# A planned two-block transformer kernel: linear attention rewritten around shifted weights, causal maxima taken four heads at a time, and the instruction order stored as a table

## The chip, the cores and the metric

The kernel runs on one core of one Trainium2 chip. The metric is device time in microseconds (us) of one launch. The host only lays the arrays out. Five engines work in parallel: TensorE (PE in the profile, with its weight loads as PEld), VectorE (DVE), ScalarE (ACT), GpSimd (POOL) and SyncE (SP), which issues the DMAs. Each runs its own instructions in order and waits on semaphores for the others. TensorE and the engines exchange results through PSUM (eight banks of 512 fp32 columns in this kernel); GpSimd is used on SBUF alone here.

## The reference

Eight sequences of 512 rows and 128 features pass four sublayers, each behind a layer norm without weights and each added to its input. Cut to what matters:

```python
x = x + L0_attn(layernorm(x))      # linear attention, 16 heads of 64, elementwise form
x = x + L0_ffn(layernorm(x))       # SwiGLU with blockwise FP4 rounding of x, h and the weights
x = x + L1_attn(layernorm(x))      # causal softmax attention, 16 heads of 8
x = x + L1_ffn(layernorm(x))       # RMS norm, top 2 of 8 LoRA experts on shared weights

def L0_attn(x):
    q, k, v = x @ wq + bq, x @ wk + bk, x @ wv + bv      # (8, 512, 16, 64) each
    Q, K = elu(q) + 1, elu(k) + 1
    KV   = sum over s of K * v                           # one number per batch, head, feature
    Ksum = sum over s of K
    attn = Q * KV / (Q * Ksum + 1e-6)
    return gelu(attn @ wo + bo)

def L1_attn(x):                
    a = (q @ k.T) / sqrt(8);  a = where(causal mask, a, -max)
    return softmax(a) @ v @ Wout
```

All arithmetic is fp32 (the expert masks are bf16, exact).

## The kernel before, in words

`block_kernel` (L745) doesn't issue instructions directly. Every call on the proxy engines is recorded as a `Step` by `Engine.__getattr__` (the lambda around L537 leads to `Plan.add`, L190), and issued at the end from `Plan.issue`. That is why nearly every row of the profile has one line, L407: it is the `getattr(e, method)(*a, **k)` in `issue`. Groups are told apart by the names of their tiles (`ahead`, `pair`, `mid` are PSUM; `kf`, `qf`, `z`, `r`, `act`, `qa`, `pr`, `mx` and so on are SBUF).

`Plan.ordered` (L249) chooses the order: a list scheduler on an estimate of each step's cost, with ranks from the table `TURNS` (one pair of numbers for each stage of each lane: loads, norm, linear, out, fp4, attention, routing, experts). A step marked `either` goes to GpSimd or VectorE, whichever the scheduler finds free first. `Plan.kept_warm` (L365) puts filler matmuls on `zeros` into gaps that the plan shows on TensorE. Sequences overlap: while one is in attention and experts, the next ones are in linear attention and the feed-forward.

Each sequence goes through these stages, with the features in 128-row chunks and the 512 rows as columns:

- `linear_attention` (L978). For each of eight chunks of 128 features, `features` (L993) makes k, v and q with one fp32 matmul of 512 columns each. `elu` (L982) adds the bias by ScalarE twice, once in a Relu into SBUF and once in an Exp in place in PSUM, then VectorE takes `min(exp - 1, relu)` and, for k, the sum `ks`. So `kf` and `qf` hold elu without the 1, which is added later: to `ks` by a one-element step, to `qf` by an Identity with bias `one_sb`. VectorE multiplies k by v (`kv`), ScalarE makes `z = q * ks + eps` and scales the chunk of `wo` (`wk_o`). `products` (L1015) handles chunks in pairs, so that one reciprocal `r` of `z0 * z1` serves two: five products on `either`, two reciprocals of 256 columns on VectorE.
- `linear_out` (L1031): eight accumulated matmuls `wk_o` by `qf`, GELU, transposes, residual.
- `fp4_feed_forward` (L1100) with `quantised` (L1054): a chain of reductions, products and bit operations on VectorE and `either`.
- `causal_attention` (L1336): four groups of four heads for each sequence, 32 in all, in `group` (L1286). The scores are taken transposed, so the row maxima must be known first. `largest` (L1210) makes the maxima of the next group, query block by query block (t = 0 to 3, with 128, 256, 384, 512 keys): matmuls of q by k for two heads in row strips 0 to 31 and 64 to 95 of TensorE, a mask added by bf16 matmuls of `mask_q` by the identity, and one VectorE reduction over 512 to 1024 elements. `to_queries` (L1236) sends the maxima as two extra rows into the q tile, `scores` (L1255) multiplies with them, ScalarE exponentiates, GpSimd masks the diagonal block, and four matmuls in column strips multiply by v (`va`) into `mid`.
- `routed` (L1356) and `experts` (L1428): 24 matmuls of 512 columns into pairs of `ahead` tiles, tanh on ScalarE, two VectorE steps, one product on `either`, then the down projection.

PSUM is two pairs of banks (`pair`), one `mid`, three `ahead`; an `ahead` tile may also take half of a pair while another pair stays open.

Of the kernel before, what the change touches and what calls it, by code (L numbers as in the profile page):

```python
# [9 lines left out]
F32 = mybir.dt.float32  # L10
F32R = mybir.dt.float32r
BF16 = mybir.dt.bfloat16
U32 = mybir.dt.uint32
AF = mybir.ActivationFunctionType
# [97 lines left out]
class Buf:  # L112


    def __init__(self, tag=None, place=None):
        self.tag, self.place = tag, place
        self.writer, self.readers = None, []
        self.first, self.users = None, {}


class Step:


    def __init__(self, number, engine, lane):
        self.number, self.engine, self.rank, self.lane = number, engine, 0.0, lane
        self.calls, self.needs, self.takes, self.uses = [], {}, [], {}
        self.cost, self.slow, self.port, self.size = 0.0, 0.0, False, 0
        self.work = 0.0
        self.start = self.end = None


TWO_PORTS = ("tensor_tensor", "scalar_tensor_tensor", "tensor_scalar", "tensor_copy")


class Plan:
# [3 lines left out]
    HOP = {"tensor": 0.1, "gpsimd": 0.1, "vector": 0.1, "scalar": 0.1, "sync": 0.2}  # L139

    def __init__(self, nc):
        self.nc, self.steps, self.open = nc, [], None
        self.lane, self.tags, self.psum, self.warmer = None, {}, (), None
        self.parts = {}
        self.engines = {n: Engine(self, n) for n in (*self.HOP, "either")}


    def tag(self, name, places, parts=None):

        self.tags[name] = list(places)  # L150
        self.parts[name] = parts or [((name, i),) for i in range(len(places))]
# [24 lines left out]

    def fixed(self, place):
        return View(Buf(place=place), place.shape)

# [4 lines left out]
    def together(self):  # L184
        return Together(self)

    def span(self, lane, low, high):
        return Span(self, lane, low, high)

    def add(self, engine, method, a, k):  # L190
        step = self.open
        if step is None:
            step = Step(len(self.steps), engine, self.lane)
            self.steps.append(step)
        elif step.engine is None:
            step.engine = engine
        assert step.engine == engine
        out = [k["out"]] if "out" in k else [a[0]]
        ins = [x for x in (*a[0 if "out" in k else 1 :], *k.values()) if isinstance(x, View)]
        if k.get("accum_out") is not None:  # L200
            out.append(k["accum_out"])
        step.calls.append((method, a, k))
        fast = "vector" if engine == "either" else engine
        if method is not None:
            step.cost += cost(fast, method, out[0], ins, a, k)
        if engine == "tensor" and method is not None:
            step.work += work(method, ins, a, k)
        if engine == "sync":
            step.size += 4 * out[0].shape[0] * _free(out[0])
        if engine == "either":  # L210
            step.slow += cost("gpsimd", method, out[0], ins, a, k)

        if engine == "gpsimd" and method != "memset":
            step.port = True
        elif engine in ("vector", "either") and method in TWO_PORTS:
            two = sum(v.shape[-1:] != (1,) or len(v.shape) > 2 for v in ins) > 1
            step.port |= (two or _free(out[0]) > 16) and not any(
                v.buf.tag in self.psum for v in (*ins, out[0]) if isinstance(v, View)
            )
        for v in ins:  # L220
            if all(v is not o for o in out) and isinstance(v, View):
                self.reads(step, v.buf)
        for v in out:
            if isinstance(v, View):
                self.writes(step, v.buf)

    def reads(self, step, buf):
        assert buf.writer is not None or buf.tag is None
        if buf.writer is not None and buf.writer is not step:
            step.needs[buf.writer] = True  # L230
        buf.readers.append(step)
        self.used(step, buf)

    def writes(self, step, buf):
        for s in (buf.writer, *buf.readers):
            if s is not None and s is not step:
                step.needs[s] = True
        buf.writer, buf.readers = step, []
        if buf.first is None and buf.tag is not None:
            buf.first = step  # L240
            step.takes.append(buf)
        self.used(step, buf)

    def used(self, step, buf):
        buf.users[step] = True
        step.uses[buf] = True


    def ordered(self):  # L249

        free = Free(self.parts)
        slots = {}
        left = {s: len(s.needs) for s in self.steps}
        then = {s: [] for s in self.steps}
        for s in self.steps:
            for n in s.needs:
                then[n].append(s)
        users = {}  # L260
        for s in self.steps:
            for b in s.uses:
                users[b] = len(b.users)
        ready_at = {s: 0.0 for s in self.steps}
        empties = set()
        for s in self.steps:
            for b in s.uses:
                if b.tag in self.psum and s.engine != "tensor" and (False or max(b.users, key=lambda u: u.number) is s):
                    empties.add(s)
        waiting = {e: [] for e in self.engines}  # L270
        for s in self.steps:
            if not left[s]:
                waiting[s.engine].append(s)
        turns = {}
        for s in sorted(self.steps, key=lambda s: (s.rank, s.number), reverse=True):
            for b in s.takes:
                turns.setdefault((s.lane, b.tag), []).append(b)
        busy = dict.fromkeys(self.engines, 0.0)
        port = 0.0
        moved = 0.0  # L280
        ends = []
        now, done, order, stuck = 0.0, 0, [], False
        clock = Clock()
        while done < len(self.steps):
            for e in self.HOP:
                while busy[e] <= now:
                    best, kept = None, set()
                    shared = waiting["either"] if e in ("vector", "gpsimd") else []
                    ready = [s for s in (*waiting[e], *shared) if ready_at[s] <= now]
                    ahead = HURRY if e == "tensor" and clock.idle(now) else 0.0  # L290
                    for s in sorted(
                        ready,
                        key=lambda s: (s.rank - (ahead if s.work > 0.6 * s.cost else 0.0) - (EMPTY if s in empties else 0.0), s.number),
                    ):
                        if s.port and port > now:
                            continue
                        asked = {}
                        for b in s.takes:
                            asked.setdefault(b.tag, []).append(b)
                        if not all(  # L300
                            all(b in turns[s.lane, t][-len(bs) :] for b in bs)
                            for t, bs in asked.items()
                        ):
                            continue
                        if all(
                            (t not in kept or stuck) and free.has(t, len(bs)) for t, bs in asked.items()
                        ):
                            best = s
                            break

                        kept.update(asked)
                    if best is None:
                        break
                    if any(
                        now < ready_at[s] <= now + PATIENCE and s.rank < min(best.rank - MARGIN, LIMIT)
                        for s in (*waiting[e], *shared)
                    ):
                        break
                    s, stuck = best, False
                    waiting[s.engine].remove(s)  # L320
                    if s.engine == "either":
                        s.engine = e
                        s.cost = s.slow if e == "gpsimd" else s.cost
                    for b in s.takes:
                        slots[b] = free.take(b.tag)
                        turns[s.lane, b.tag].remove(b)
# [1255 lines left out]
```

## Time and profile before

| what | before |
|---|---|
| median of 3 runs (lowest, highest) | 1126.88 us (1125.94, 1127.14) |
| the profiled execution: its span from first to last instruction | 1130.1 us |
| TensorE busy, granted clock | 1040.2 us, 0.982 in the mean |
| VectorE, ScalarE, GpSimd busy | 830.3, 630.8, 624.3 us |
| instructions TensorE, VectorE, ScalarE, GpSimd | 5025, 1868, 1084, 669 |
| first attention matmul, last group's output | 172 us, 1065 us |
| filler matmuls on `zeros` | 40.4 us busy |
| DMA | 44.3 MB, 11.9% of 16 engines |

The page gives no time of the profiled execution other than its span. It is 0.3% above the median of the runs, so a time worked out from the profile is multiplied by 1126.88 / 1130.1. An fp32 matmul stands as two records in the profile. "Busy" for TensorE is the union of records whose ends are modelled and overlap the next start: a matmul of 512 columns has a record of 0.5 to 0.6 us where the next starts 0.43 us later. GpSimd, VectorE and ScalarE records overlap the next one by some 0.05 to 0.1 us too. All work that the plan marked `either` ran on GpSimd in the kernel before.

### The profile page before, as it was taken

What the parts mean: (1) busy time and instruction counts of PE and PEld (TensorE: products, weight loads), DVE (VectorE), ACT (ScalarE), POOL (GpSimd) and SP (SyncE); (2) the same over time, 40 slices, a digit from 0 to 9 for tenths busy, and PEclk for the clock granted to TensorE, in tenths of its full rate; (3) what the DMA queues carried; (4) which work ended last, traced back from release to release, by engine and by line L of the source; (5) the groups of instructions that cost most, each with busy time, mean ns of one, the idle gap of its engine ahead of it and who ended that gap; (6) DMA issues with size and microseconds to landing.
All of it is one profiled execution on the core that took longest, in us unless ns stands there. A gap on an engine that the chain in (4) does not pass through costs nothing.

```text
span 1130.1 us, 15043 instructions
## 1 busy us (share of the span) xinstructions
PE 1040.2 (92%) x5025; PEld 488.0 (43%) x5025; DVE 830.3 (73%) x1868; ACT 630.8 (56%) x1084; POOL 624.3 (55%) x669
## 2 busy tenths in 40 slices
PE   6667788998899999999998999999999999999998
PEld 2223333344344444444543444454454445445454
DVE  6868879897888967758788968788667765556543
ACT  5756787678786644644578555764443443344311
POOL 6647846676676466237635755467644533441534
PEclk9879989999999999999999999999999999999999
DMA  8000030001101020111012000210002102001000
GB/s 235 1 1 0 1 111 1 21 20 56 39 20 30 10 94 20 58 72 35 26 39 94 19 21 20 95 30 19 20 7 98 39 20 104 21 20 30 1 10 9
DMA packets 30572, 44.31 MB, mean 39 GB/s; under 512 B 4192, under 2 KB 18464, under 8 KB 30496
## 3 DMA queue, kind: packets, MB, share of 16 engines
q1 hardware_dynamic: 30496, 43.37, 11.9%
q8 instruction: 39, 0.64, 0.2%
q14 instruction: 37, 0.30, 0.1%
HBM read 23.95 MB, written 18.87 MB: 38 GB/s over the span
## 4 chain that ended last, share of the span: by engine, by line
PE 57%; DVE 15%; ACT 6%; issue 2%; POOL 1%; DMA 0%; POOLq 0%; DVEq 0%; ACTq 0%
PE ahead L407 31%; PE pair L407 19%; PE mid L407 7%; ACT pr L407 2%; DVE r L407 2%; DVE mx L407 2%; DVE h L407 1%; DVE sc L407 1%; ACT qf L407 1%; DVE s4 routing L407 1%; DVE qf L407 1%; DVE act L407 1%; ACT z L407 1%; DVE kf L407 1%; DVE oh L407 1%
## 5 line engine op out<-in xcount | busy, mean ns | idle before, releaser
L407 ACT ACTIVATE pr<-pair 128x1024 f32<-128x1024 f32 (+1 forms) x192 | 166.7, 879 | 149.2 <-PE pair L407 129.1
L407 DVE TENSOR_REDUCE mx<-pair 128x4 f32<-128x512 f32 (+2 forms) x192 | 198.5, 1041 | 68.4 <-PE pair L407 57.7
L407 POOL TENSOR_SCALAR_AFFINE_SELECT pr<-pr 128x256 f32<-128x256 f32 (+1 forms) x192 | 92.8, 485 | 176.4 <-ACT pr L407 175.6
L407 PE MATMUL pair<-qkT 32*128 32x128 f32 (+7 forms) x1024 | 172.3, 387 | 9.4 <-ACT pr L407 2.7
L407 PEld LDWEIGHTS pair<-qkT 32*128 32x128 f32 (+1 forms) x1024 | 84.4, 183 | 181.8 <-ACT pr L407 52.0
L407 POOL TENSOR_TENSOR act<-act,tw 128x512 f32<-128x512 f32 x64 | 81.3, 1272 | 88.8 <-DVE act L407 80.6
L407 PE MATMUL ahead<-um,b_sb 128*128 128x512 f32 x240 | 122.2, 607 | 0.0
L407 DVE RECIPROCAL r<-r 128x256 f32<-128x256 f32 x64 | 110.3, 1736 | 14.9 <-POOL r L407 14.8
L407 DVE SCALAR_TENSOR_TENSOR act<-act,ahead 128x512 f32<-128x512 f32 x120 | 81.9, 684 | 51.4 <-ACT act L407 38.0
L407 POOL TENSOR_TENSOR qa<-qa,qa 128x704 f32<-128x704 f32 (+4 forms) x60 | 81.2, 1354 | 35.1 <-DVE qa L407 26.2
L407 POOL TENSOR_TENSOR qf<-qf,r 128x512 f32<-128x512 f32 x64 | 80.5, 1278 | 34.5 <-DVE r L407 27.8
L407 PE MATMUL mid<-pr,va 128*10 128x512 f32 (+3 forms) x1024 | 93.3, 435 | 0.0
L407 POOL TENSOR_TENSOR qf<-qf,z 128x512 f32<-128x512 f32 x64 | 80.3, 1270 | 0.0
L407 ACT ACTIVATE act<-ahead 128x512 f32<-128x512 f32 x60 | 35.8, 597 | 72.0 <-PE ahead L407 71.9
L407 PE MATMUL ahead<-act,a_sb 128*128 128x512 f32 x128 | 65.2, 619 | 0.0
L407 POOL TENSOR_TENSOR r<-z,z 128x512 f32<-128x512 f32 x32 | 40.9, 1278 | 41.6 <-ACT z L407 39.3
L407 PE MATMUL ahead<-tT,w_sb 128*128 128x512 f32 x120 | 63.3, 609 | 0.0
L407 ACT ACTIVATE ahead<-ahead,bqkv_sb 128x512 f32<-128x512 f32 x96 | 63.0, 656 | 0.0
L407 PE MATMUL pair<-mask_q,ident 128*128 128x128 bf16 (+1 forms) x384 | 61.6, 242 | 0.0
L407 PE MATMUL ahead<-xnT,wk 128*128 128x512 f32 x100 | 56.7, 650 | 4.8 <-DVE kf L407 2.1
L407 PEld LDWEIGHTS ahead<-um,b_sb 128*128 128x128 f32 x240 | 40.7, 190 | 36.1 <-issue 29.6
L407 ACT ACTIVATE z<-qf,eps_sb,s 128x512 f32<-128x512 f32 x64 | 51.9, 811 | 6.8 <-DVE s L407 5.1
(227 smaller groups left out, 1986.4 us busy)
## 6 DMA issues: line engine op xcount, KB each, us to landing
stacks<-qk SPq DMA_DIRECT2D x32, 512.0 KB
qkT<-stacks SPq DMA_DIRECT2D x128, 128.0 KB
x<-in SPq DMA_DIRECT2D x8, 256.0 KB
qkT<-mr SPq DMA_DIRECT2D x128, 4.0 KB
out<-x SPq DMA_DIRECT2D x8, 256.0 KB
w_sb<-in SPq DMA_DIRECT2D x3, 256.0 KB
wq<-in SPq DMA_DIRECT2D x4, 128.0 KB
wk<-in SPq DMA_DIRECT2D x4, 128.0 KB
```

Of the source, the lines that this page charges most:

```text
L407: getattr(e, method)(*a, **k)
```

## The change

Five parts go together.

1. *Order as a table.* `Step` and `Plan` lose costs, ranks and the scheduler; `issue` reads the order of all steps from a string `ORDER`, the engine of each `either` step from `ENGINES` (147 on VectorE, 229 on GpSimd), the buffer of each tile from `PLACES`, and twelve filler matmuls from `ZEROS`. PSUM is three pairs, one `mid`, one `ahead`, and an `ahead` tile may be any half of a pair. Some pools change their number of buffers.
2. *Biases and the 1 in shifted weights.* The last feature of a layer norm's output follows from the other 127, so that row of `xnT` is set to 1 (by the scale and bias of the copy out of PSUM), and twelve matmuls at the start make weights whose last row carries the bias, plus 1 for q and k. The projections then come out of TensorE with the bias and the 1 in them.
3. *One Exp a projection.* `elu + 1` is `max(p, min(exp(p - 1), 1))`: for k one Exp and one VectorE step (which also sums), for q one Exp and two VectorE steps.
4. *Quotient as kv/ks less a small term.* `Q KV / (Q ks + eps)` is `KV/ks * (1 - eps / (Q ks + eps))`. The first factor goes into `wk_o`, now on VectorE. The second is a reciprocal of `z`, taken for four chunks at once: nine products on `either` and two reciprocals of 256 columns for four chunks.
5. *Four-head maxima and mask factors.* The four heads of a group lie in the four row strips of TensorE; the causal mask is a product of two 32-row bf16 factors (`causal_factors`), also in four strips. Query blocks 0 and 1 share a step. The maxima of the two i-parts need one more tiny minimum, and `scores` takes 64 rows instead of 34 for one of the parts.

```diff
-    places("pair", [P, 2, 512], 2, pool=sums)
+    places("pair", [P, 2, 512], 3, pool=sums)
     places("mid", [P, 512], 1, pool=sums)
-    places("ahead", [P, 512], 3, pool=sums)
+    places("ahead", [P, 512], 1, pool=sums)
...
-    def issue(self):
-        for s in self.ordered():
+    def issue(self, order, engines, places, zeros):
+        engine = iter(engines)
+        for s in self.steps:
+            if s.engine == "either":
+                s.engine = {"v": "vector", "g": "gpsimd"}[next(engine)]
...
+        for at, n in enumerate(numbers):
+            s = self.steps[n]
             for b in s.takes:
-                b.place = self.tags[b.tag][self.slots[b]]
+                b.place = self.tags[b.tag][int(next(place), 36)]
+            if at in zeros:
+                self.warmer(zeros[at])
             e = getattr(self.nc, s.engine)
...
+    def shifted_weights():
+        nc.vector.tensor_scalar(
+            shift_b[:, 31, 0:16], bqkv_sb[:, 0:2].rearrange("p i c -> p (i c)"), 1.0, None, ALU.add
+        )
+        nc.vector.tensor_copy(shift_b[:, 31, 16:24], bqkv_sb[:, 2])
+        for part in range(4):
+            for i in (1, 2, 0):
+                w = wqkv[i][part]
+                pw = new("ahead", [P, 256])
+                with one_go():
+                    nc.tensor.matmul(pw, shift, w, start=True, stop=False, skip_group_check=True)
+                    for j in range(2):
+                        nc.tensor.matmul(
+                            pw[96:128, ts(j, P)], shift_b[:, :, 8 * i + 2 * part + j], ident,
+                            start=False, stop=True, skip_group_check=True,
+                        )
+                nc.scalar.copy(w, pw)
...
-            nc.scalar.activation(f, pw, AF.Relu, bias=bias)
-            nc.scalar.activation(pw, pw, AF.Exp, bias=bias)
-            nc.vector.scalar_tensor_tensor(f, pw, -1.0, f, ALU.add, ALU.min, **accum)
...
+        def keys(c):
+            ks, kv, rk = (new("s1", [P, 1]) for _ in range(3))
+            pw = projection(1, c)
+            kf = new("kf", [P, S])
+            nc.scalar.activation(kf, pw, AF.Exp, bias=minus_sb)
+            nc.vector.scalar_tensor_tensor(kf, pw, 1.0, kf, ALU.max, ALU.min, accum_out=ks)
+            nc.vector.scalar_tensor_tensor(
+                kf, kf, 1.0, projection(2, c), ALU.mult, ALU.mult, accum_out=kv
+            )
+            nc.vector.tensor_scalar(rk, ks, 1e-30, None, ALU.max)
+            nc.vector.reciprocal(rk, rk)
+            wk_o = new("wk_o", [P, D])
+            nc.vector.tensor_scalar(
+                wk_o, wo_sb[c // 2][:, c % 2, :], kv, rk, ALU.mult, ALU.mult
+            )
+            return ks, wk_o
+
+        def denominator(c, ks):
+            pw = projection(0, c)
+            z = new("qf", [P, S])
+            nc.scalar.activation(z, pw, AF.Exp, bias=minus_sb)
+            nc.vector.tensor_scalar(z, z, -1.0, 0.0, ALU.add, ALU.min)
+            nc.vector.scalar_tensor_tensor(z, z, 1.0, pw, ALU.add, ALU.max)
+            nc.scalar.activation(z, z, AF.Identity, bias=eps_sb, scale=ks)
+            return z
...
-            (q0, z0, w0), (q1, z1, w1) = features(c), features(c + 1)
-            r = new("r", [P, S])
-            nc.either.tensor_tensor(r, z0, z1, ALU.mult)
-            nc.either.tensor_tensor(q0, q0, z1, ALU.mult)
-            nc.either.tensor_tensor(q1, q1, z0, ALU.mult)
+            ab, cd, r = (new("r", [P, S]) for _ in range(3))
+            nc.either.tensor_tensor(ab, zs[0], zs[1], ALU.mult)
+            nc.either.tensor_tensor(cd, zs[2], zs[3], ALU.mult)
+            nc.either.tensor_tensor(r, ab, cd, ALU.mult)
             for part in (slice(0, 256), slice(256, S)):
                 nc.vector.reciprocal(r[:, part], r[:, part])
-            nc.either.tensor_tensor(q0, q0, r, ALU.mult)
-            nc.either.tensor_tensor(q1, q1, r, ALU.mult)
+            nc.either.tensor_tensor(cd, cd, r, ALU.mult)
+            nc.either.tensor_tensor(ab, ab, r, ALU.mult)
+            for z, other in zip(zs, (cd, cd, ab, ab)):
+                nc.either.tensor_tensor(z, z, other, ALU.mult)
+                nc.scalar.activation(z, z, AF.Identity, scale=-1e-6, bias=one_sb)
...
-    def stack(h):
-        return slice(64 * h, 64 * h + 32)
+    def stack(i, h):
+        return slice(64 * h + 32 * i, 64 * h + 32 * i + 32)
...
     def largest(n, t, mx):
...
+        t = max(t, 1)
+        some = (1, 0) if t == 1 else (t,)
+        w = sum((u + 1) * P for u in some)
+        pairs = [new("pair", [P, 2, 512]) for _ in range(2)]
+        four = [(i, h) for h in range(2) for i in range(2)]
+        with one_go():
+            for u in some:
+                for i, h in four:
...
+                    nc.tensor.matmul(
+                        to, duo(n, i)[stack(i, h), 0, ts(u, P)], keys,
+                        start=(u == t), stop=False, skip_group_check=True,
+                    )
+            k = len(some)
+            for i, h in four:
+                nc.tensor.matmul(
+                    pairs[i][:, h, w - k * P : w].rearrange("p (k c) -> p k c", k=k),
+                    mask_q[stack(i, h)],
+                    mask_k[stack(i, h)].unsqueeze(1).to_broadcast([32, k, P]),
+                    start=False, stop=True, skip_group_check=True,
+                )
...
-                        rows = slice(64 * h, 64 * h + 34)
+                        rows = slice(64 * h, 64 * h + (64 if i else 34))
```

## The prediction

> **What bounds the kernel now.** I read the page first: busy time by engine, then the 40 slices.
>
> ```profile
> PE 1040.2 (92%) x5025; PEld 488.0 (43%) x5025; DVE 830.3 (73%) x1868; ACT 630.8 (56%) x1084; POOL 624.3 (55%) x669
> PE   6667788998899999999998999999999999999998
> DVE  6868879897888967758788968788667765556543
> ```
>
> TensorE leads, but not everywhere: in the first third VectorE is as busy as TensorE. So next I asked for busy time by stretch. I cut where the fourth and the 24th attention group write `on` (337.3 and 896.4 us), because both kernels pass these points with nearly the same work behind them. The columns are stretch, length, then busy time (and count) of PE, PEld, DVE, ACT, POOL, then the granted clock.
>
> ```profile
> 0.00:337.30 337.30, 276.34 (x1020) 122.45 (x1020) 272.78 (x659) 240.97 (x427) 220.85 (x239) 0.95 0.14 42
> 337.30:896.40 559.10, 540.25 (x2865) 257.57 (x2864) 429.12 (x944) 311.86 (x532) 315.61 (x333) 1.00 0.13 42
> 896.40:1130.10 233.70, 223.65 (x1143) 107.96 (x1142) 128.43 (x265) 77.93 (x126) 87.80 (x98) 0.99 0.09 28
> ```
>
> Stage A (337.3 us): VectorE 81% and TensorE 82%, and of TensorE's 276 us 24 are filler matmuls on `zeros`. Each of the four engines is filled to 65 to 82%, so waits between engines set the pace, with VectorE the one with least room. Stage B (559.1): TensorE 97%, VectorE 77%. Stage C (233.7): TensorE 96%. In B and C a microsecond taken from TensorE is a microsecond of the kernel until VectorE is full.
>
> Third, the groups by form: prices of what goes and what comes (busy, mean ns of one).
>
> ```profile
> L407 DVE RECIPROCAL r<-r 128x256 f32<-128x256 f32 x64 | 110.3, 1736 | 14.9 <-POOL r L407 14.8
> L407 DVE TENSOR_TENSOR x<-ahead,x 128x512 f32<-128x512 f32 x8 | 5.5, 690 | 3.3 <-PE ahead L407 3.3
> L407 DVE TENSOR_SCALAR y<-y 128x512 f32<-128x512 f32 x8 | 3.3, 417 | 2.2 <-ACT y L407 2.2
> L407 ACT ACTIVATE wk_o<-wo,s 128x128 f32<-128x128 f32 x64 | 25.1, 394 | 9.5 <-DVE s L407 6.3 <-PE ahead L407 3.1
> L407 POOL TENSOR_TENSOR qf<-qf,z 128x512 f32<-128x512 f32 x64 | 80.3, 1270 | 0.0
> ```
>
> Last, TensorE's timeline at a maxima step, since means of a pipelined engine overlap and only start-to-start times add up (start, length, instructions):
>
> ```profile
> 706.68 0.49 PE L407 MATMUL pair<-qkT 32*128 32x512 f32 x2
> 707.11 0.28 PE L407 MATMUL pair<-mask_q,ident 128*128 128x128 bf16 x2
> 707.32 0.62 PE L407 MATMUL mid<-pr,va 128*10 128x256 f32 x8
> ```
>
> Two heads' matmuls of 512 columns, in two row strips, take 0.43 us together (706.68 to 707.11). The two mask matmuls behind them take 0.21 here, 0.12 at most other places (66 and 56 ns from start to start).
>
> **The change, part by part.** The counts are from the built instruction orders of both kernels.
>
> *Maxima on TensorE.* Start-to-start times of a pair in the trace are 0.172, 0.211, 0.370 and 0.428 us for 128, 256, 384 and 512 columns. A group needs two pairs of each: 2.36 us. Its masks are eight of 128 columns (0.061 each) and four of 256 (0.115 each): 0.95 us. After, four heads stand in four strips and four banks. If four run in the time of two, the first term halves: 1.18 saved. The masks become 32-row matmuls in four strips: 0 to 0.71 saved, depending on whether the strips overlap. No row shows four row strips at once. The nearest is the attention-times-value step with four column strips, whose four matmuls start 6 to 7 ns apart, so I take overlap for the maxima and about half of it for the masks: 1.5 us a group, 48 us in all (bounds 0 and 60). VectorE's reductions stay at 192 instructions and 5120 elements a group (198.5 us): nothing there.
>
> A rule speaks for caution here. The Trainium skill, "TensorEngine Tiling (Array Packing)", section "PSUM Bottleneck", says that row tiling speeds up the matmul but not the copying out, which may then be the bottleneck. By it alone the maxima step would be worth nothing, because the reduction of 1.22 us for two heads is longer than the 0.64 us of matmuls before it. The row that decides is stage B, with TensorE at 97% and VectorE at 77%: other matmuls take the freed time.
>
> *Shifted weights.* Twelve times a 256-column fp32 matmul (half of the 0.86 of a 512-column one, 0.43), two of 128 (0.11 each) and a ScalarE copy of about 0.35: 8 us on TensorE, 4 on ScalarE, once, in stage A.
>
> *Linear attention on ScalarE.* 128 Relu of 685 ns go (-88), 64 `wk_o` scalings go (-25), 12 copies come: -108 us, 631 to about 523. The Identity behind the quotients takes the place of the one behind `qf`.
>
> *On VectorE.* 32 of 64 reciprocals go: -56. There come 64 tensor_scalar on `qf` at 417 (+27), 64 `wk_o` scalings, about 0.28 each by the 270 ns of the one-element row with two scalars (+18), 32 tiny minima and some 25 set-up steps (+12). The small `s` steps change by -5. And 147 tensor_tensor that all ran on POOL move over: 112 of 512 at 690 (+77), 25 of 704 at some 0.95 (+24), 10 smaller (+5). The sum is +102 by means; engine time is about 0.8 to 0.9 of means, because the next instruction starts some 80 ns before the last ends, so +82: 830 to 912. By place in the built order +20 fall in stage A, +33 in B, +28 in C.
>
> *On POOL.* 118 products of 512 go at 1.27 (-150), 35 longer or equal ones of `quantised` and ten smaller ones (-58): 624 to about 420.
>
> *Contention.* VectorE now has some 210 more instructions that read SBUF alone while POOL works there. The row: the eight `y<-y,y` on VectorE last 681 ns at least, 684 in the median and 1082 once, and the mean is 734. One in eight stretched by 0.4 us makes 210 x 0.05 = 10 us; all of them would be 84. I take +8 by that row, since POOL is busy two fifths of the time.
>
> The Trainium skill, "GPSIMD Engine Reference", section 8, "Key points", says that POOL shares its SBUF interfaces with VectorE and contends with two-input VectorE instructions, which speaks against moving products over. By it each moved product could be stretched; the one row in eight is what this trace shows.
>
> *Filler and clock.* 44 filler matmul steps become 12. They stand in gaps and are worth 0 to 6 us after stage A. Against that, the clock: in stage A the grant is 0.95, and fewer fillers could lower it. A grant of 0.90 would cost TensorE some 14 us in A, where it is not alone on the path: 0 to +10, taken at +2.
>
> *Order, PSUM.* The order at run time is now a table in the source. PSUM is three pairs and one single bank instead of two and three, and single tiles take half-pairs, so up to seven of them can be open. Where both orders pass the 4th and the 24th group, TensorE's need counted with the same prices differs by -3 in A, -44 in B and about 0 in C (where more of the experts' work now lies): -47 in all, which is -48 and fillers left out, +8 for the weights, and rounding between stages.
>
> **The sum**, against the profiled 1130.1 us. A: VectorE 273 + 20 = 293 busy; it was idle 64 us, waiting mostly on POOL and ScalarE (`r` 10.2, `kf` 10.0 us), which are 35 and 17% lighter; I take 37 idle: 330. B: 559 - 44 = 515, VectorE then at (429 + 33) / 515 = 90%, so I add 5 of new waits for it: 520. C: -2, a last stage with more free engines: 232. Together 1082. Runs stand to the profiled execution as 1126.88 to 1130.1, so 1079 us.
>
> **Rivals.** *Better packed*: with ScalarE and POOL light, VectorE idles only 20 us in A (313), TensorE's idle time in B halves from 19 (506) and C loses its 10 us of idle time (222): 1041, 1038 as run. For it: twelve fillers instead of 44, so the recorded order sees few gaps on TensorE. Against: VectorE would have to be over 91% busy in A and B, and its best 100 us so far were 88.
>
> *Strips that don't overlap four at a time*: only some of the masks' time is saved (B 548), with A 335 and C 236: 1119, 1116 as run. For it: no row shows four row strips. Against: the four column strips.
>
> *Slower: VectorE as the bound.* It decides if VectorE cannot be kept busy over 84% in A and B, where it now has 293 + 462 = 755 us (755 / 896). At the shares it had, 81% in A and 82% in the fullest late 100 us of B, A takes 362 and B 565: 1161, 1158 as run. For it: products and scalings move to the engine that had least room in A. Against: what it waited for in A is exactly what gets lighter.
>
> *The moved work is hidden and nothing changes*: would need TensorE's 97% in B to be no bound.
>
> **How the numbers follow.** Forecast (1050 to 1100) 0.50; better packed 0.25; strips 0.13; VectorE as the bound 0.10; no change 0.02. The range goes from 1026 (the better-packed case with another 12 us out of A) to 1118 (strips). Faster by over 0.2% (about what three runs of this kernel can tell from no change: they span 1.2 us) 0.88, within it 0.02, slower 0.10.
>
> **What would show it.** Maxima: four `qkT` matmuls starting within some 20 ns of each other and the next step 0.43 us later; if the second pair starts 0.4 us after the first, the strips don't overlap. VectorE near 912 us, 88 to 90% in A and B; ScalarE near 523, POOL near 420, no group `kf<-ahead,bqkv_sb`. TensorE near 960 busy. Two-input VectorE products well over 0.75 us in the mean would mean contention; a clock under 0.93 in A, that the fillers were needed. The prediction is wrong if A takes over 350 us or B over 545.

## The result, and the profile after

The changed kernel takes 1248.1 us in the median of four runs (1246.6 to 1252.3), beside 1127.0 for the kernel before in the same comparison: 1.1055 times as long (95% interval 1.1018 to 1.1092). The forecast was 1079, and the time lies above the whole range. The profiled execution spans 1250.5 us.

The page after, busy time by engine and the slices of TensorE and VectorE:

```profile
PE 1035.2 (83%) x5033; PEld 485.0 (39%) x5033; DVE 916.6 (73%) x2166; ACT 549.0 (44%) x904; POOL 439.4 (35%) x522
PE   5867677988888898777988788997879998989987
DVE  6678878787868478687787578778768977567545
```

No engine is full. TensorE's busy time hardly moved, but the span grew by 120 us: TensorE now idles 215 us (1250.5 less 1035.2) where it idled 90. The work sums of the prediction came out within 5% on three engines: VectorE 917 (912 forecast), ScalarE 549 (523), GpSimd 439 (420). So the lost time is, for the most part, not work; it is waiting.

The stages after, cut 10.8 us behind the fourth and the 24th write of `on`. (The cuts of the prediction, 337.3 and 896.4, also lie 10.8 us behind those writes, which end at 326.4 and 885.6; the text there names the writes themselves. The stages of both kernels are cut alike, so they compare.)

```profile
0.00:377.10 377.10, 290.50 (x1028) 129.25 (x1028) 288.07 (x788) 182.04 (x305) 147.26 (x185) 0.89 0.12 38
377.10:999.00 621.90, 524.12 (x2837) 248.42 (x2836) 475.44 (x1067) 283.49 (x466) 223.49 (x255) 0.95 0.11 38
999.00:1250.50 251.50, 220.62 (x1177) 107.28 (x1169) 153.06 (x313) 83.46 (x135) 68.64 (x82) 0.97 0.08 26
```

Most is lost in stage B: 622 us instead of 559, with TensorE at 84% (97% before) and VectorE at 76% (77% before). The granted clock fell too, to 0.89 in A.

Who is waited for, from the waits of TensorE's weight loads after (total us, times, longest):

```profile
PEld pair L214 <- DVE mx L214: 65.8, 80, 2.7
PEld pair L214 <- DVE act L214: 53.3, 39, 6.9
PEld pair L214 <- ACT pr L214: 51.0, 73, 1.4
PEld pair L214 <- DVE kf L214: 44.7, 33, 4.2
PEld pair L214 <- DVE on L214: 21.5, 16, 6.8
```

The rows that grew are waits of `pair` for VectorE: no row for `act` or `on` stood among the first before, and the one for `mx` was half as long:

```profile
PEld pair L407 <- DVE mx L407: 33.9, 52, 1.3
```

In the chain of waits VectorE's share went from 15% to 35% and TensorE's from 57% to 51%, although VectorE is idle a quarter of the time. That does not look like a full engine. One of the `on` waits shows what it is. The timeline after, at the ninth `on` (start, length, instruction, idle time before it and what ended it):

```profile
502.94 0.47 PEld L214 LDWEIGHTS pair<-ident,oT 128*128 128x128 f32 x4 [0.33 <-issue]
503.05 0.60 PE L214 MATMUL pair<-ident,oT 128*128 128x128 f32 x4
...
503.69 0.26 DVE L214 RECIPROCAL rz<-pair 128x16 f32<-128x16 f32 x1 [1.04 <-PE pair L214]
...
505.34 0.28 DVE L214 TENSOR_TENSOR on<-pair,rz 128x128 f32<-128x128 f32 x1
...
505.68 1.20 PE L214 MATMUL pair<-xnT,wq 128*128 128x512 f32 x2 [2.03 <-DVE on L214]
```

TensorE stands still for 2.03 us until VectorE has written `on`. But the matmul behind the wait is a q projection of linear attention, of another sequence, and has nothing to do with `on`. In the built instruction order this matmul writes columns 512 to 1023 of `pair_1`, the second bank, and the `on` step reads columns 0 to 487 of `pair_1`, the first bank. No address is shared. They are tied because both banks are one tile of `[P, 2, 512]`: the software layer that puts in the semaphore waits orders the accesses to such a PSUM tile as if they met.

I call this a half-wait, and counted them: every TensorE wait in the built order, traced to the instruction that releases it, and kept if the two touch the same tile but no common address. There are 46 before and 232 after. Of the 232, 50 are released by steps that write `act`, 47 by steps that write `kf` and 16 by `on`, and none by a maxima reduction (`mx`) or an exponential of the scores (`pr`): the rows of `mx` and `pr` above are waits for the bank itself. (ScalarE and VectorE have such waits as well, 53 and 37 before, 52 and 46 after; it is TensorE's that multiply.) With three pairs of two banks and one single bank, nearly all single tiles live in halves of pairs, and TensorE can seldom fill one half while another engine empties the other.

### The profile page after: what moved, and what is told of

Same layout as the page of the kernel before. It is cut to its first block, busy times and chain, and to the rows that moved or that the text cites. A ratio compares the mean times of both kernels' runs of the same rounds, so it can differ in the third digit from the quotient of the medians.

```text
span 1250.5 us, 14914 instructions
## 1 busy us (share of the span) xinstructions
PE 1035.2 (83%) x5033; PEld 485.0 (39%) x5033; DVE 916.6 (73%) x2166; ACT 549.0 (44%) x904; POOL 439.4 (35%) x522
## 4 chain that ended last, share of the span: by engine, by line
PE 51%; DVE 35%; ACT 8%; issue 4%; POOL 2%; DMA 0%; SPq 0%; ACTq 0%; DVEq 0%; POOLq 0%
PE pair L214 40%; DVE mx L214 8%; PE ahead L214 7%; DVE kf L214 4%; DVE qf L214 4%; DVE act L214 3%; PE mid L214 3%; DVE r L214 3%; DVE qa L214 2%; ACT pr L214 2%; ACT qf L214 1%; DVE sc L214 1%; DVE x L214 1%; DVE wk_o L214 1%; DVE h L214 1%
## 5 line engine op out<-in xcount | busy, mean ns | idle before, releaser
L214 DVE TENSOR_REDUCE mx<-pair 128x6 f32<-128x768 f32 (+2 forms) x192 | 193.2, 1037 | 39.6 <-PE pair L214 38.4
L214 PE MATMUL pair<-qkT 32*128 32x256 f32 (+11 forms) x1024 | 141.1, 402 | 30.8 <-DVE mx L214 12.4
L214 PEld LDWEIGHTS pair<-qkT 32*128 32x128 f32 (+2 forms) x1024 | 70.6, 194 | 179.3 <-DVE mx L214 60.0
L214 PE MATMUL pair<-um,b_sb 128*128 128x512 f32 x180 | 99.3, 641 | 19.2 <-DVE act L214 10.3
L214 DVE SCALAR_TENSOR_TENSOR act<-act,pair 128x512 f32<-128x512 f32 x90 | 60.9, 682 | 62.0 <-PE pair L214 34.5
L214 PE MATMUL pair<-xnT,wv 128*128 128x512 f32 x110 | 68.2, 711 | 23.2 <-DVE kf L214 5.4
L214 PE MATMUL pair<-xnT,wk 128*128 128x512 f32 x112 | 65.8, 676 | 20.9 <-DVE kf L214 9.8
L214 PE MATMUL pair<-xnT,wq 128*128 128x512 f32 x98 | 58.0, 681 | 13.3 <-DVE s L214 3.4
L214 PE MATMUL pair<-qf,wk_o 128*128 128x512 f32 x96 | 52.0, 668 | 16.1 <-DVE on L214 5.9
L214 DVE RECIPROCAL r<-r 128x256 f32<-128x256 f32 x32 | 54.9, 1732 | 0.1
```

## The experiments

Theories: **half-waits** (the declaration of PSUM), against **the recorded order**, **VectorE's load and contention**, **too few banks** (a maxima step takes four at once), **long chains** of the new linear attention, and, later, **the split instructions** of the remedy itself. The first four runs separate the parts; the others bear on the half-waits. "Scheduler" means `Plan.ordered` of the kernel before, with its ranks as they were.

**The order table** (e1). All new arithmetic and the new PSUM layout, ordered by the scheduler:

```diff
-        plan.issue(ORDER, ENGINES, PLACES, ZEROS)
+        plan.issue()  # costs, ranks and scheduler of before
```

> All the new computation and the new PSUM layout (three pairs, one single bank), but ordered by the scheduler of the kernel before, with its TURNS ranks (one more stage for the weights) and its cost model (four-strip matmuls priced at half). Recorded-order theory (the table fits other durations than the chip's, so the engines wait in a bad sequence): 1080 to 1120 us, TensorE waiting less than in the changed kernel. PSUM theory (the maxima step takes two pairs at once and single tiles sit in halves of pairs): 1200 to 1270, the waits of TensorE on VectorE's mx, act and kf stay. Linear-attention theory (four chunks at a time lengthen the chain): 1200 to 1270 as well, told apart by the next two kernels.

Measured: 1280.1 us, 1.1315 (1.1265 to 1.1364), just above every range that was expected. The recorded order is not at fault; it is some 30 us better than the scheduler's.

**Linear attention alone** (e2), with the old maxima and the old PSUM layout, scheduler:

```diff
     def linear_attention(b):   # as changed: keys, denominator, shifted weights
...
     places("pair", [P, 2, 512], 2, pool=sums)   # as before
```

> Only the new linear attention with its shifted weights, under the scheduler before, with two-head maxima and the PSUM layout before. Linear-attention theory: 1180 to 1250, and stage A (up to the fourth group) is longer than 360 us. Recorded-order theory: 1100 to 1140. PSUM theory: 1090 to 1130.

Measured: 1204.1 us, 1.0643 (1.0591 to 1.0695), in the range of the linear-attention theory. But its sign, a stage A of over 360 us, did not come: the fourth write of `on` ends at 318.8 us (326.4 before). The time is lost behind it: the 24th write ends at 949.3 us (885.6 before).

**Four-head maxima alone** (e3), with their PSUM layout and the old linear attention, scheduler:

```diff
-    places("pair", [P, 2, 512], 2, pool=sums)
+    places("pair", [P, 2, 512], 3, pool=sums)
...
-    places("ahead", [P, 512], 3, pool=sums)
+    places("ahead", [P, 512], 1, pool=sums)
...
     def largest(n, t, mx):   # as changed
```

> Only the four-head maxima and mask factors, with the new PSUM layout, under the scheduler before, with the linear attention before. PSUM theory: 1170 to 1250, with TensorE waiting on mx for over 60 us. Recorded-order theory: 1070 to 1110. Linear-attention theory: 1070 to 1110.

Measured: 1249.9 us, 1.1048 (1.0949 to 1.1146). The part that should take work from TensorE loses more than the other when it stands alone, and it is the part that brings the layout. TensorE's weight loads wait for `mx` only 30 us, not over 60 as the theory of the layout had it; most of the loss is not a wait for the maxima.

**Products back on GpSimd** (e4). The changed kernel with the 147 products that had moved to VectorE on GpSimd again:

```diff
-ENGINES = ("gggvvg..."    # 147 v, 229 g
+ENGINES = ("gggggg..."    # 376 g
```

> The changed kernel with its order table, but the 147 products that the table gives to VectorE run on GpSimd as before. Contention theory (VectorE's two-input products collide with GpSimd on SBUF and VectorE is late everywhere): VectorE falls to about 800 us busy, its tensor_scalar on qf from 455 to about 420 ns, and the time to 1150 to 1210. Recorded-order theory: 1240 to 1320, since GpSimd's 1.27 us come into a sequence made for 0.6. PSUM theory: 1240 to 1300.

Measured: 1253.7 us, 1.1081 (1.103 to 1.1132), with VectorE at 859.5 us instead of 916.6. Taking 57 us from VectorE gains nothing, so its load does not hold this kernel. Contention did not go with the products: with GpSimd busy 611 us instead of 439, the tensor_scalar on `qf` takes 559 ns instead of 455 (about 420 was expected). With that much more of it the time moves by under 0.5%, so contention does not hold the kernel either.

**The changed kernel, banks apart** (e5). Same table, engines and places; each pair is two tiles of one bank, and the instructions that read both banks become two:

```diff
-    places("pair", [P, 2, 512], 3, pool=sums)
+    plan.tag("pair", [
+        Two([
+            sums.tile([P, 512], F32, name=f"pair_{i}_{h}", tag=f"pair_{i}_{h}")
+            for h in range(2)
+        ])
+        for i in range(3)
+    ])
...
-            nc.vector.tensor_reduce(to, heads, AX.X, ALU.max, negate=True)
+            with one_go():
+                for h in range(2):
...
+                    nc.vector.tensor_reduce(to, heads, AX.X, ALU.max, negate=True)
```

> The changed kernel with the same order table, engines and places, but each PSUM pair is declared as two tiles of one bank instead of one tile of two. The 192 maxima reductions and the 192 exponentials of the scores, which read both banks, become two instructions of one bank each, and so do the 16 copies of q and k. Half-wait theory: in the changed kernel 232 TensorE waits are for work on the other bank of the same pair, and here none is, so a large part of TensorE's excess idle time (215 us against 90 before) goes: 1130 to 1190 us, and TensorE's waits for maxima reductions and linear-attention steps halve. Rival, too few banks whatever their declaration (a maxima step takes four of eight at once): 1235 to 1265 us, since nothing but extra instructions is new. Rival, the long chains of linear attention: also 1235 to 1265 us.

Measured: 1080.8 us (1080.2 to 1085.4), 0.9558 (0.9534 to 0.9582) of the kernel before: 167 us less than the changed kernel and faster than both. That is below the 1130 to 1190 that the half-wait theory expected, and 2 us from the forecast of the prediction (by ratio 0.9558, where 1079 to 1126.88 is 0.9575). Its page, TensorE above all:

```profile
PE 992.5 (92%) x5033; PEld 482.6 (45%) x5033; DVE 929.0 (86%) x2366; ACT 560.5 (52%) x1104; POOL 441.8 (41%) x522
PE   5987687998899999999999999998899999999998
```

Its stages, cut like the others:

```profile
0.00:318.70 318.70, 264.60 (x1037) 121.81 (x1038) 292.66 (x824) 184.10 (x336) 148.39 (x185) 0.96 0.14 45
318.70:851.90 533.20, 511.82 (x2828) 251.57 (x2828) 479.94 (x1190) 290.62 (x589) 224.38 (x255) 0.97 0.13 44
851.90:1078.40 226.50, 216.04 (x1173) 109.19 (x1169) 156.43 (x354) 85.80 (x180) 69.05 (x82) 0.99 0.09 29
```

TensorE idles 86 us (1078.4 less 992.5), less than before the change, and its clock is back at 0.96 in A with the same twelve fillers. The waits of its weight loads:

```profile
PEld pair L225 <- DVE mx L225: 62.9, 113, 1.9
PEld pair L225 <- ACT pr L225: 42.4, 81, 1.0
...
PEld pair L225 <- DVE act L225: 22.5, 27, 6.9
...
PEld pair L225 <- DVE kf L225: 17.6, 26, 3.5
```

`act` and `kf` fall to about two fifths, and `on` from 21.5 us to 7.7. `mx` stays at 63 us, and I had expected it to halve: those are true waits, for banks that the reductions still read. VectorE's share of the chain of waits is 41% here, more than the 35% of the changed kernel, so that share was no sign of half-waits. And the ninth `on` again, in the timeline of this run:

```profile
429.82 1.02 PE L225 MATMUL pair<-xnT,wq 128*128 128x512 f32 x2
...
430.68 1.02 PE L225 MATMUL pair<-xnT,wk 128*128 128x512 f32 x2
...
431.68 0.28 DVE L225 TENSOR_TENSOR on<-pair,rz 128x128 f32<-128x128 f32 x1
```

The same q projection now starts 1.86 us before the `on` step that it waited for.

**The split without the declaration** (e9). The kernel of e5 with pairs declared as one tile again, and nothing else:

```diff
-    plan.tag("pair", [Two([...]) for i in range(3)])
+    places("pair", [P, 2, 512], 3, pool=sums)
```

> The kernel of the run with banks apart (1080.8 us), with the same split instructions, order and places, but each pair declared again as one tile of two banks. Only the declaration differs. Half-wait theory: TensorE has 529 waits for work on the other bank of a pair (the split instructions add some to the 232), so 1235 to 1290 us. Rival, the split instructions themselves brought the gain, since a reduction or an exponential of one bank starts earlier and frees its bank earlier: 1075 to 1130 us.

Measured: 1255.4 us, 1.1118 (1.107 to 1.1166). Built, it has on every engine the same instructions in the same order at the same PSUM addresses as e5; only the waits differ. The declaration alone makes 175 us. The waits show it:

```profile
PEld pair L225 <- DVE mx L225: 67.5, 82, 2.8
PEld pair L225 <- ACT pr L225: 55.4, 76, 1.7
PEld pair L225 <- DVE act L225: 53.9, 39, 6.9
PEld pair L225 <- DVE kf L225: 44.4, 34, 4.2
...
PEld pair L225 <- DVE on L225: 22.2, 16, 6.8
```

These are the rows of the changed kernel again. The count is 529 where it was 232, and the time is nearly the same: not the number of half-waits but where they fall sets their price.

**The kernel before, banks apart** (e6): the same edit on its two pairs, scheduler.

> The kernel before with its own scheduler and two pairs, each pair declared as two tiles of one bank; instructions over both banks become two. Half-wait theory: before has 46 TensorE waits for the other bank of a pair, a fifth of the changed kernel's 232, so there is little to win: 1105 to 1130 us, less what some 400 more instructions cost VectorE and ScalarE off TensorE's path. Rival, the extra instructions cost and the waits never mattered: 1130 to 1150 us.

Measured: 1132.6 us, 0.9991 (0.9962 to 1.002). The 46 half-waits before cost nothing that shows, net of the extra instructions (VectorE +22 us, ScalarE +13). The time lies in the range of the rival, 3 us past that of the half-wait theory, and this run can't tell a small gain that the extra instructions eat from none. So the remedy is no improvement in general; it cures what the change brought.

**The layout alone** (e7): the kernel before with nothing but the new numbers of pairs and single banks.

```diff
-    places("pair", [P, 2, 512], 2, pool=sums)
+    places("pair", [P, 2, 512], 3, pool=sums)
...
-    places("ahead", [P, 512], 3, pool=sums)
+    places("ahead", [P, 512], 1, pool=sums)
```

> The kernel before with its own arithmetic, scheduler and maxima, and only the PSUM layout of the change: three pairs and one single bank, single tiles in halves of pairs, each pair one tile of two banks. 158 TensorE waits are for the other bank of a pair, against 46. Half-wait theory: the layout alone costs much, 1170 to 1250 us. Rival, the cost lies in the new maxima and the new linear attention: 1115 to 1140 us.

Measured: 1235.4 us, 1.0912 (1.0894 to 1.093), with 158 half-waits. Without any of the new arithmetic, the layout costs 103 us (1132.0 for the kernel before in the same comparison), nearly what the change lost. The scheduler plans another order for this layout, and it was not run with banks apart, so how much of the 103 us is half-waits is not shown. Its page shows the same signs, TensorE at 87% and no engine above it:

```profile
PE 1074.0 (87%) x5053; PEld 497.5 (40%) x5053; DVE 843.7 (68%) x1868; ACT 638.5 (52%) x1084; POOL 624.4 (51%) x669
```

**All new parts under the scheduler, banks apart** (e8; e1 with the edit of e5).

> All of the new arithmetic and the new PSUM layout, ordered by the scheduler of before (this took 1280 us with pairs of one tile), with each pair declared as two tiles of one bank. The scheduler counts the two banks of a pair as independent, which is now true. Half-wait theory: 1140 to 1200 us. Rival, too few banks or long chains: 1265 to 1300 us.

Measured: 1161.6 us, 1.0263 (1.0244 to 1.0281): 118 us less than e1, and 81 more than e5, which computes the same in the recorded order. Of these 81 us not all are the order: the scheduler leaves nearly all products on GpSimd (612 us busy), and e12 below prices that at 24 us in the recorded order.

**The maxima alone, banks apart** (e10; e3 with the edit of e5).

> Four-head maxima, mask factors and the new PSUM layout with the old linear attention, ordered by the scheduler of before (1249.9 us with pairs of one tile), now with pairs of two tiles. The prediction priced the maxima at 48 us of TensorE's time. Half-wait theory with that price: 1080 to 1125 us. If taking two whole pairs at a time costs as much as it saves: 1125 to 1170 us. Rival, the layout is not what costs: 1235 to 1260 us.

Measured: 1129.0 us, 0.9982 (0.9965 to 1.0): 121 us less than e3, but no gain over before: in the range that says taking two whole pairs at a time costs as much as it saves, not in that of the forecast price. The scheduler put 88.4 us of filler matmuls into gaps of its plan, against 40.4 before; so part of the time that TensorE saves may have become gaps of that plan. Which of the two it is stays open.

**Linear attention alone, banks apart** (e11; e2 with the edit of e5, two pairs and three single banks).

> The new linear attention alone with the old maxima and the old PSUM layout (two pairs and three single banks), ordered by the scheduler of before, pairs of two tiles. With pairs of one tile it took 1204.1 us with only 54 TensorE waits for the other bank, so these can't be its whole loss. If its loss is the longer chains of four chunks under ranks made for two, the time stays at 1185 to 1210 us; if the waits are the loss, 1120 to 1150 us.

Measured: 1185.3 us, 1.0486 (1.0453 to 1.0518), 19 us less than e2. Most of its loss under the scheduler is a different one. Filler matmuls are at 88.6 us, so the plan itself had more gaps; whether they come from the longer chains or from ranks made for the old ones is not settled by these runs. In the recorded order the same code is part of the fastest kernel.

**Products on GpSimd, banks apart** (e12; e5 with the edit of e4).

> The kernel of the run with banks apart (1080.8 us) with the 147 products that its table puts on VectorE moved back to GpSimd. In the changed kernel this made no difference (1253.7 against 1248.1 us). Here VectorE is 86% busy and in the middle over 90%. If VectorE's load and its contention with GpSimd hold this kernel: 1060 to 1078 us. If TensorE does, and the products' delay on GpSimd (1.3 us instead of 0.75) shows: 1081 to 1105 us.

Measured: 1105.3 us, 0.9774 (0.9743 to 0.9806): 24 us more than e5, where the same edit on the changed kernel made no difference that can be told (1253.7 beside 1248.1). The time is at the upper end of the range for products delayed on GpSimd. Once TensorE is free of half-waits, dividing the products between the two engines gains 24 us. Whether moving them back costs this by the longer products on GpSimd or by the VectorE instructions that GpSimd's work stretches (below) is not separated.

| kernel | half-waits | us | banks apart, us |
|---|---|---|---|
| before | 46 | 1127 | 1133 (e6) |
| layout alone (e7) | 158 | 1235 | not run |
| linear attention alone, scheduler (e2) | 54 | 1204 | 1185 (e11) |
| maxima alone, scheduler (e3) | 169 | 1250 | 1129 (e10) |
| all, scheduler (e1) | 162 | 1280 | 1162 (e8) |
| all, recorded order: the change | 232 | 1248 | 1081 (e5) |
| the same, split instructions (e9) | 529 | 1255 | 1081 (e5) |

Times are medians, each with its own runs of the kernel before beside it (1127 to 1132 us). With banks apart the count is 0 in every row. The four kernels with the new layout that were run both ways are 118 to 175 us faster with banks apart, those with the old layout at most 19. Only e9 and e5 differ by the declaration alone; in the other rows the split instructions come with it, and where the scheduler orders, it plans anew.

## Why the prediction was wrong

The step that failed is "Order, PSUM". It noted three pairs and one single bank, and that single tiles take half-pairs, "so up to seven of them can be open", and gave this no price. Seven could be open by address, but not for TensorE: the built order had 232 waits of one half for the other. This step should have carried some +170 us (167 by the change less e5, 175 by e9 less e5). It was open to a reader before the run: the projection that waits for `on` stands in the built order of the changed kernel, but that order was read for work, not for waits. The rule on PSUM that was weighed, from the Trainium skill, "TensorEngine Tiling (Array Packing)", section "PSUM Bottleneck", says that after the speedup by tiling the copying out of PSUM may become the bottleneck. What was lost here was not the speed of copying: in e5 the reductions take 205 us instead of 193 and the kernel is faster by 13%.

The other steps can be judged on e5, where the half-waits are gone:

- *The sum and the stages*: 330, 520 and 232 forecast, 318.7, 533.2 and 226.5 measured; 1082 against 1078.4. That the sum agrees so closely is partly luck: A is 11 us shorter than forecast (VectorE idles 26 us there, 37 were taken) and B 13 us longer. In the changed kernel A took 377 and B 622, past the bounds (350 and 545) at which the prediction called itself wrong.
- *Maxima*: the overlap was right, and the price nearly. By start times in the changed kernel's trace, four heads' matmuls of 512 columns begin within 10 ns of each other and the mask follows 0.343 us after the first (two heads: 0.4315 before). From a step's first matmul to the next one behind its masks, the medians of a group's steps add up to 2 x 0.555 + 2 x 0.498 + 0.601 + 0.708 = 3.41 us before and to 0.507 + 0.453 + 0.822 = 1.78 in e5, waits included: 1.6 us a group or 52 in all. The shortest of each step add up to 3.33 and 1.45: 1.9 us a group or 60 in all. 48 was forecast. The timeline of the changed kernel at such a step:

```profile
630.00 0.50 PE L214 MATMUL pair<-qkT 32*128 32x512 f32 x4
630.34 0.23 PE L214 MATMUL pair<-mask_k,mask_q 32*128 32x128 bf16 x4
630.50 1.13 PE L214 MATMUL pair<-um,b_sb 128*128 128x512 f32 x2
```

- *VectorE*: 912 forecast, 917 measured in the changed kernel. Within it the `wk_o` scalings were sized too small (0.28 us each) and the products too (0.69):

```profile
L214 DVE TENSOR_SCALAR qf<-qf 128x512 f32<-128x512 f32 x64 | 29.0, 455 | 6.5 <-ACT qf L214 6.4
L214 DVE TENSOR_SCALAR wk_o<-wo,s,s 128x128 f32<-128x128 f32 x64 | 27.0, 430 | 0.1
L214 DVE TENSOR_TENSOR act<-act,tw 128x512 f32<-128x512 f32 x29 | 23.4, 808 | 0.3
```

- *Contention*: the 112 products of 512 columns that moved to VectorE (such as the last row above) last 0.771 us in the mean in the changed kernel's trace, so by the prediction's own sign there is contention, some 9 us on them. The 73 that no product or mask step of GpSimd overlaps last 0.683 us in the mean and 0.693 at most, the other 39 0.935 in the mean. It costs no time that shows in the changed kernel (e4), and moving the products back costs 24 us in e5 (e12). The rule that was weighed, from the Trainium skill, "GPSIMD Engine Reference", section 8, "Key points", that GpSimd shares its SBUF interfaces with VectorE and contends with VectorE instructions of two SBUF inputs, is seen in these durations but did not decide against the move.
- *Filler and clock*: the clock fell to 0.89 in A, which the prediction had named as the sign that the fillers were needed. That reading falls: e5 has the same twelve fillers and 0.96. The grant was lower where TensorE stood still more: it is busy 77% of A in the changed kernel and 83% in e5.
- *TensorE near 960*: 992.5 in e5. The same matmuls count 1035.2 us in the changed kernel, so busy time holds some waiting or slower clock, and I can't say what of the 32 us is work.
- *Rivals*: the slower one, VectorE as the bound, is refuted by e4 for the changed kernel: VectorE was not kept busy because it too waited. It was the wrong mechanism for a slower result. Strips that don't overlap: refuted by the start times. *Better packed* did not come either.
- *Slips of the working*, which decide nothing: the cuts lie 10.8 us behind the writes that the text names; GpSimd gets 33% lighter by its own 624 and 420, not 35%; and -48 for the maxima with +8 for the weights makes -40, so the -47 leaves 7 us to fillers and rounding that no line shows.

What stays open: how the 51 us by which e5 is faster than before (1132.0 in the same comparison) divide between maxima and linear attention. Neither gains alone under the scheduler, whose ranks were made for the kernel before, and the recorded order is for both together.

## What to carry to other kernels

When a PSUM tile spans more than one bank and single tiles are lent its parts, look in the built order at which waits are for the other bank: they cost nothing in a sum of work, and here they turned a gain of 4% into a loss of 11%. Declare a tile for each bank and accept a second instruction where one read both; the 384 extra reductions and exponentials here cost some 12 us on each of two engines (VectorE 86% busy with them, ScalarE 52%). And a control that changes only the declaration (e9) tells such a remedy apart from what else it brings.

## What was not expected of the hardware

At 512 columns the step behind four row strips of 32 rows starts sooner than the one behind two did: 0.343 us after the first matmul for four heads, 0.4315 for two. That four strips are themselves faster is not shown, since what follows differs: a mask matmul in 32 rows after, in 128 rows before. At 256 columns, where matmuls in strips follow in both kernels, it is 0.223 us in the median of either.

GpSimd at work also stretches VectorE instructions that read one large operand from SBUF. With GpSimd busy 442 us the `wk_o` scaling takes 438 ns in the mean (e5); with 612 us it takes 601 ns (e12), for the same 128 columns. In e12 the 25 scalings that no product or mask step of GpSimd overlaps take 346 ns at most, and the 15 during which such steps run throughout take 968 in the mean. The groups by form, of e5 first and then of e12:

```profile
L225 DVE TENSOR_SCALAR wk_o<-wo,s,s 128x128 f32<-128x128 f32 x64 | 27.6, 438 | 0.1
...
L225 DVE TENSOR_SCALAR wk_o<-wo,s,s 128x128 f32<-128x128 f32 x64 | 38.0, 601 | 0.2
L225 DVE TENSOR_SCALAR qf<-qf 128x512 f32<-128x512 f32 x64 | 34.2, 538 | 2.9 <-ACT qf L225 2.8
```
